# Half of one gate's products in bf16 parts, in four recurrent steps of eight

## The chip, the cores and the metric

One Trainium2 chip, one of its cores. The metric is the device time of one launch in microseconds; the kernel before was run three times and the median is taken. A profile is one more execution of the same program, recorded by the hardware.

## What is computed

The reference is a gated recurrent cell over 512 time steps, 8 sequences and 512 units, all in fp32, with the input added to the output at the end:

```
def step(h, x_t):
    fused = sigmoid(concat([x_t, h]) @ w_W + w_b)      # (8, 1024) @ (1024, 1024)
    hidden_state, output_state = split(fused, 2)        # r and z, 512 columns each
    memory_state = x_t @ wx_W + wx_b + hidden_state * (h @ wh_W + wh_b)
    h_new = output_state * h + (1.0 - output_state) * tanh(memory_state)
    return h_new, h_new
_, hs = scan(step, h0, swapaxes(x, 0, 1))
return x + swapaxes(hs, 0, 1)
```

Step i needs all 512 units of h from step i-1, so the steps cannot overlap as a whole. The products with x do not depend on h and can be made ahead.

## The kernel before

**Layout.** The 512 units stand as 4 blocks of 128 partitions. The stationary operand of every product with h is one block k of the state (32 columns: 4 steps of 8 sequences share a tile, and the current step fills 8 of the 32). The moving operand is a piece of the weights. The output goes to one quarter of 32 partitions of a PSUM bank: `tile_position` (0, 32j) with j = 0 to 3. So each product is four matmuls, one for each quarter j of the tensor array's columns, and the four quarters work side by side. A profile counts two records (two weight loads and two streams) for each fp32 matmul.

**Banks.** The 384 output columns of a step lie in three banks. A (192 columns) holds h, z and r for the first half of the units ("half A"); B (128 columns) holds r and h for half B; C (64 columns, in the tile `cs`) holds z for half B. On the tensor engine (PE) a step runs in this order, where the letter is the bank and the digit the block k of the state:

```
ORDER = "A0 B0 A1 A2 A3 B1 B2 B3 C0 C1 C2 C3"
```

After C3 come the products with x that belong to later steps (`x_step`, tiles `xp` and `eps`). They are spread over the steps by a table: in steps u = 0 to 3 of every eight, each quarter of the array takes 384 columns of them, in steps u = 4 to 7 it takes 288.

**The rest of a step.** The vector engine (DVE) transposes each piece out of PSUM (`tr`, `md1`, `tz`), the scalar engine (ACT) applies the sigmoids and tanh, and DVE scans compute the memory state (`m`) and the new state. The new state has four pieces, one for each block k: `update(0, 0)` and `update(0, 1)` write blocks 0 and 1 (tile hTA), `update(1, 0)` and `update(1, 1)` blocks 2 and 3 (tile hTB). A0 and B0 of the next step wait for block 0, A1 for block 1, A2 for block 2, A3 for block 3. GpSimd (POOL) adds x to the new state for the output (`ot`) and makes sums of x (`sx`).

**Seeding.** Before a group of four steps starts, its banks are filled with the x products and the bias: `spread` copies them with ACT, bank C by one copy of 64 columns in step u = 7 (for even groups) or u = 1 (for odd ones). All four steps of a group add their h products to the same region, each in rows of its own.

**Order.** The program is written in order by hand. `Flow` records the instructions, and its `plan` gives each one the semaphore waits that its reads, its writes and the PSUM banks require, within one engine too. The order on each engine is that of the code.

## Time and profile before

| | |
|---|---|
| median of 3 runs | 1654.62 us (1654.59 to 1654.87) |
| the profiled execution's own time | 1657.46 us, span 1655.7 us |
| busy in the span | PE 1645.6, PE weight loads 1500.2, DVE 1153.9, ACT 1193.8, POOL 301.9 us |
| PE matmul records | 54298, as many weight loads |
| granted PE clock | 0.999 |

Times in the rows are microseconds from the start of the span; the last number of a group's row is the mean of one instruction in ns. Matmul records overlap: a record's length includes the way through the array, so the distance from one start to the next tells how long the array was taken up. "PEld" is the weight load. A bracket at a row's end names what the engine waited for just before. Where two shapes of a step are compared, u is the step's place in its eight.

### The profile page before, as it was taken

The numbers are of one execution on the slowest core, as the hardware profiler recorded it, in microseconds if no ns is written. First come the engines' busy times: TensorE is split into PE (matmuls) and PEld (weight loads), VectorE is DVE, ScalarE is ACT, GpSimd is POOL, SyncE is SP. The second block draws the span as 40 slices with busy tenths as digits, with TensorE's granted clock in tenths as the row PEclk, the third lists the DMA queues.
The fourth block names the chain that finished last, engine by engine and source line by source line (L and its number), as shares of the span: only waits on it lengthen the run. The fifth ranks groups of instructions, "written<-read, shape, count | busy, mean of one in ns | idle before, by whom it ended". The sixth has DMA issues, their size and how long they took to land.

```text
span 1655.7 us, 125580 instructions
## 1 busy us (share of the span) xinstructions
PE 1645.6 (99%) x54298; PEld 1500.2 (91%) x54298; DVE 1153.9 (70%) x9194; ACT 1193.8 (72%) x5998; POOL 301.9 (18%) x1279
## 2 busy tenths in 40 slices
PE   9999999999999999999999999999999999999998
PEld 5999999999999999999999999999999999999987
DVE  6776676676766766767667767677676766766765
ACT  3777777777777777777777777777777777777775
POOL 1211111111111111111111111111111111111111
PEclk9999999999999999999999999999999999999999
DMA  4000000000000000000000000000000000000000
GB/s 182 11 18 14 15 15 16 16 14 15 16 15 15 14 16 16 14 14 15 16 15 14 14 17 14 15 14 17 14 14 15 17 14 14 15 17 10 10 10 10
DMA packets 37284, 31.14 MB, mean 19 GB/s; under 512 B 4084, under 2 KB 35060, under 8 KB 36600
## 3 DMA queue, kind: packets, MB, share of 16 engines
q1 hardware_dynamic: 36576, 22.89, 4.5%
q8 instruction: 424, 6.95, 1.7%
q14 instruction: 132, 1.08, 0.2%
q10 hardware_dynamic: 152, 0.22, 0.1%
HBM read 14.70 MB, written 8.39 MB: 14 GB/s over the span
## 4 chain that ended last, share of the span: by engine, by line
PE 99%; DVE 1%; issue 0%; ACT 0%; DVEq 0%; SPq 0%
PE A L227 40%; PE B L227 26%; PE xp L227 18%; PE cs L227 13%; PE eps L227 1%; DVE tr L227 0%; DVE m L227 0%; DVE tz L227 0%; DVE md1B L227 0%; DVE md1A L227 0%; DVE hTA L227 0%; DVE hTB L227 0%; ACT hTB L227 0%; DVE zeros L227 0%; DVE rows L227 0%
## 5 line engine op out<-in xcount | busy, mean ns | idle before, releaser
L227 PE MATMUL A<-wa,hTA 128*32 128x192 f32 x8192 | 559.5, 326 | 2.4 <-DVE hTA L227 2.2
L227 PE MATMUL B<-wb,hTA 128*32 128x128 f32 x8192 | 454.8, 273 | 0.0
L227 PE MATMUL A<-wa,hTB 128*32 128x192 f32 x8192 | 448.6, 326 | 0.0
L227 PEld LDWEIGHTS A<-wa,hTA 128*32 128x32 f32 x8192 | 292.5, 122 | 124.6 <-DVE hTA L227 101.7
L227 DVE STREAM_TRANSPOSE tr<-A 128x64 f32<-128x64 f32 x512 | 128.0, 250 | 367.6 <-PE A L227 367.6
L227 POOL TENSOR_TENSOR ot<-xin,hTB 128x16 f32<-128x16 f32 x495 | 123.8, 250 | 1290.4 <-DVE hTB L227 1290.4
L227 PEld LDWEIGHTS B<-wb,hTA 128*32 128x32 f32 x8192 | 352.6, 122 | 2.8 <-issue 0.3
L227 PE MATMUL B<-wb,hTB 128*32 128x128 f32 x8192 | 339.6, 273 | 0.0
L227 PEld LDWEIGHTS A<-wa,hTB 128*32 128x32 f32 x8192 | 330.4, 122 | 9.1 <-DVE hTB L227 0.2
L227 ACT ACTIVATE md0A<-tr 128x16 f32<-128x16 f32 x512 | 112.4, 219 | 238.5 <-DVE tr L227 238.4
L227 PE MATMUL xp<-tw,sx 128*32 128x384 f32 (+2 forms) x1464 | 269.7, 433 | 0.0
L227 PEld LDWEIGHTS B<-wb,hTB 128*32 128x32 f32 x8192 | 262.3, 122 | 0.2 <-issue 0.2
L227 PE MATMUL cs<-wb,hTB 128*32 128x64 f32 x8192 | 230.3, 219 | 0.4 <-issue 0.3
L227 PE MATMUL cs<-wb,hTA 128*32 128x64 f32 x8192 | 230.2, 219 | 0.0
L227 DVE TENSOR_TENSOR_SCAN hTB<-hd0B,hTB 128x24 f32<-128x24 f32 x1024 | 158.0, 196 | 99.8 <-ACT hTB L227 99.8
L227 PE MATMUL xp<-wx,xin 128*32 128x384 f32 (+4 forms) x1348 | 219.1, 413 | 0.0
L227 PEld LDWEIGHTS cs<-wb,hTA 128*32 128x32 f32 x8192 | 207.5, 122 | 0.0
L227 DVE TENSOR_TENSOR_SCAN hTA<-hd0A,hTA 128x24 f32<-128x24 f32 x1024 | 190.9, 186 | 0.0
L227 ACT ACTIVATE hd0B<-tz 128x16 f32<-128x16 f32 x512 | 115.6, 226 | 94.5 <-DVE tz L227 94.5
L227 PEld LDWEIGHTS cs<-wb,hTB 128*32 128x32 f32 x8192 | 180.2, 122 | 0.7 <-issue 0.7
L227 ACT ACTIVATE hTB<-hTB 128x16 f32<-128x16 f32 x512 | 120.3, 235 | 79.1 <-DVE hTB L227 72.8
L227 ACT ACTIVATE hTA<-m 128x8 f32<-128x8 f32 x1024 | 160.8, 206 | 0.6 <-DVE m L227 0.3
(101 smaller groups left out, 2680.6 us busy)
## 6 DMA issues: line engine op xcount, KB each, us to landing
out_dram<-ot SPq DMA_DIRECT2D x128, 64.0 KB, 1.6
xin<-in_x_dram SPq DMA_DIRECT2D x112, 64.0 KB, 2.4
wx<-in_wx_dram SPq DMA_DIRECT2D x4, 768.0 KB, 7.0
wa<-in_wa_dram SPq DMA_DIRECT2D x4, 384.0 KB, 9.8
wb<-in_wb_dram SPq DMA_DIRECT2D x1, 1152.0 KB, 13.7
xin<-in_x_dram SPq DMA_DIRECT2D x3, 256.0 KB, 3.7
wb<-in_wb_dram SPq DMA_DIRECT2D x1, 384.0 KB, 14.1
head<-in_xh_dram ACTq DMA_DIRECT2D x1, 208.0 KB, 4.7
```

What stands on the lines that cost most here:

```text
L227: inst = getattr(self, item.op, getattr(engine, item.op, None))(*item.args, **item.kw)
```

## The change

For half B of z the change takes the fp32 product apart into bf16 parts, in the steps u = 0 to 3 from step 8 on (252 of the 512 steps: the ones where `in_parts` holds). Three parts of the state (`split`: the high 16 bits of h, of what is left, and of what is left then; 8 columns each) stand side by side as one stationary operand of 24 columns. Three parts of the weights (`wb`, `w2`, `w3`, each read as the high 16 bits of every fp32 word, so with a step of two bf16 elements) stream past it. `kept` issues a matmul that loads no weights of its own but uses those that the matmul ahead of it has loaded. Each quarter and each block k has one loading matmul and two kept ones.

The nine products land in 24 rows and are summed afterwards: each such step has a PSUM region of its own (`cell`), DVE transposes it (`tzB`) and reduces over the four row groups (`tzs`). Since a sum over all rows must hold the x product once, `spread_c` seeds a cell through a mask that keeps the eight rows of the step: four ACT instructions of 64 columns for each even group, two in u = 6 and two in u = 7, in place of one copy. POOL makes the parts of the state by two subtractions for each half, before the output's additions; it makes `w2` and `w3` once, in steps 1 to 4. On DVE the first scan of `m` for half B now stands ahead of the z work, and `update(0, 1)` behind it. The state tiles of the two halves become one tile `hs` with 32 more rows of zeros.

```
-DVE_FILL = 23
+DVE_FILL = 14
...
+    hs = [const.tile([P, NQ, 64, 3], F32, name=f"hT{i}") for i in range(NH)]
+    split = [const.tile([P, NQ, 3, B], F32, name=f"split{i}") for i in range(2)]
+    w2 = const.tile([P, NQ, NQ, HU], F32, name="w2")
+    w3 = const.tile([P, NQ, NQ, HU], F32, name="w3")
+    mask = const.tile([P, GS, 32], F32, name="mask")
...
+    def parts(out_, i, k, j):
+        lhsT = high(split[i % 2])[:, k].rearrange("p u b -> p (u b)")[:, 1::2]
+        for n, t_ in enumerate((wb[:, k, j, :HU], w2[:, k, j], w3[:, k, j])):
+            (nc.tensor.kept if n else mm)(out_, lhsT, high(t_)[:, 1::2])
...
+    def cell(i):
+        return cs[:, HU * (i % GS) : HU * (i % GS) + HU] if i // GS % 2 == 0 else banks[1]["C"]
+    def in_parts(i):
+        return NH <= i < T and i // GS % 2 == 0
+    def spread_c(g, steps_):
+        for s in steps_:
+            nc.scalar.activation(
+                cell(GS * g + s), source(g)[:, XP["C"]], AF.Copy, scale=mask[:, s, :1]
+            )
...
             for j in range(NQ):
-                mm(ps[bank][32 * j : 32 * j + 32, :], hs, wh(bank, k, j))
+                if bank == "C" and in_parts(i):
+                    parts(cell(i)[32 * j : 32 * j + 24], i, k, j)
+                else:
+                    to = cell(i) if bank == "C" else ps[bank]
+                    mm(to[32 * j : 32 * j + 32, :], lhsT, wh(bank, k, j))
...
+            if hf and in_parts(i):
+                tz = work.tile([P, 2, B], F32, tag="tzs", name=f"tzs_{i}")
+                nc.vector.tensor_reduce(
+                    tz, tzb[0].rearrange("p c (u b) -> p c b u", u=4), mybir.AxisListType.X, ALU.add
+                )
...
+        if in_parts(i):
+            tzb = [work.tile([P, 2, 32], F32, tag="tzB", name=f"tzB_{i}")]
+            nc.vector.transpose(tzb[0].rearrange("p c n -> p (c n)"), raw["z"][1])
+            memory(1, 0)
+            turn_z(1)
+            update(0, 1)
+            memory(1, 1)
...
+        if nxt and u in (6, 7):
+            spread_c(2 * o + 2, (2 * u - 12, 2 * u - 11))
         for hf in range(2):
             act(state(hf, i + 1, 0), state(hf, i + 1), AF.Copy)
+            if in_parts(i + 1):
+                ks, s1 = slice(2 * hf, 2 * hf + 2), B * ((i + 1) % GS)
+                t_, new = split[(i + 1) % 2][:, ks], hs[(i + 1) % NH][:, ks]
+                nc.gpsimd.tensor_tensor(
+                    t_[:, :, :2].rearrange("p k u b -> p k b u"),
+                    new[:, :, s1 : s1 + B, 2].unsqueeze(3).broadcast_to([P, 2, B, 2]),
+                    high(new).rearrange("p k (u n) s -> p k n u s", u=2)[:, :, s1 : s1 + B, :, 5],
+                    ALU.subtract,
+                )
+                nc.gpsimd.tensor_tensor(t_[:, :, 2], t_[:, :, 0], high(t_)[:, :, 0, 1::2], ALU.subtract)
...
-            spread(2 * o + 2, "C")
```

Three places show how the order moves. The first is PE in a step u = 1 in mid-program, from the C products over the x products (`xp`) to the next step's A products. Before:

```order
L227 MATMUL cs<-wb,hTA_68 32x64 x8
L227 MATMUL cs<-wb,hTB_76 32x64 x8
L227 MATMUL xp_122<-wx,xin_140 32x384 x2
L227 MATMUL xp_122<-tw_101,sx_107 32x384 x2
L227 MATMUL A_118<-wa,hTA_69 32x192 x4
```

After, with the first of sixteen groups of three (`w_77` and `w_78` are `w2` and `w3`):

```order
L245 MATMUL B_117<-wb,hT_68 32x128 x12
L245 MATMUL cs<-wb,split_76 24x64
L219 MATMUL cs<-w_77,split_76 24x64
L219 MATMUL cs<-w_78,split_76 24x64
...
L245 MATMUL xp_120<-wx,xin_131 32x384 x2
L245 MATMUL xp_120<-tw_99,sx_105 32x384 x2
L245 MATMUL A_116<-wa,hT_69 32x192 x4
```

Sixteen fp32 matmuls of 64 columns became sixteen groups of one loading and two kept matmuls; the x products behind them are as many as before.

The second is DVE in a step u = 2, from the transposes of bank B to the new state. Before:

```order
L227 STREAM_TRANSPOSE tr_2_145<-B_119 128x64
L227 STREAM_TRANSPOSE md1B_89<-B_119 128x64
L227 SCALAR_TENSOR_TENSOR hTA_70<-hd0A_91,hTA_69 128x24
L227 STREAM_TRANSPOSE tz_2_146<-cs 128x64
L227 SCALAR_TENSOR_TENSOR hTA_70<-hd0A_91,hTA_69 128x24
L227 SCALAR_TENSOR_TENSOR m_2_142<-md0B_85,md1B_89 128x16 x2
L227 SCALAR_TENSOR_TENSOR hTB_78<-hd0B_93,hTB_77 128x24 x2
```

After (the four pieces of the state are all in `hT`; `hd0A` and `hd0B` tell the half):

```order
L245 STREAM_TRANSPOSE tr_2_143<-B_117 128x64
L245 STREAM_TRANSPOSE md1B_86<-B_117 128x64
L245 SCALAR_TENSOR_TENSOR hT_70<-hd0A_88,hT_69 128x24
L245 STREAM_TRANSPOSE tzB_156<-cs 128x64
L245 SCALAR_TENSOR_TENSOR m_2_140<-md0B_82,md1B_86 128x16
L245 TENSOR_REDUCE tzs_157<-tzB_156 128x16
L245 SCALAR_TENSOR_TENSOR hT_70<-hd0A_88,hT_69 128x24
L245 SCALAR_TENSOR_TENSOR m_2_140<-md0B_82,md1B_86 128x16
L245 SCALAR_TENSOR_TENSOR hT_70<-hd0B_90,hT_69 128x24 x2
```

The second piece of half A's state stands two instructions later, behind one scan of `m` and the added reduce.

The third is POOL at the end of the steps u = 0 and u = 1, after (`hT_69` is the state that step u = 1 makes). Before, the two additions `ot` stood there alone:

```order
L245 TENSOR_TENSOR sx_108<-xin_145,sx_104 128x64
L245 TENSOR_TENSOR ot_124<-xin_138,hT_68 128x8x2 x2
L245 TENSOR_TENSOR split_75<-hT_69 128x2x8x2
L245 TENSOR_TENSOR split_75<-split_75 128x2x8
...
L245 TENSOR_TENSOR ot_124<-xin_138,hT_69 128x8x2 x2
```

Two pairs of subtractions (the second pair reads as the first) were put ahead of the additions; the first pair waits for half A's state, the second for half B's.

## The prediction

> **What bounds the kernel now.** I read the page's first part and its chain of waits, then the stretch of the steady steps:

> ```profile
> PE 1645.6 (99%) x54298; PEld 1500.2 (91%) x54298; DVE 1153.9 (70%) x9194; ACT 1193.8 (72%) x5998; POOL 301.9 (18%) x1279
> PE 99%; DVE 1%; issue 0%; ACT 0%; DVEq 0%; SPq 0%
> 98.00:1600.00 1502.00, 1501.92 (x49891) 1380.11 (x49887) 1050.81 (x8414) 1104.75 (x5529) 275.70 (x1174) 1.00 0.05 15
> ```

> PE is never idle there (1501.92 of 1502 us), at the full clock (1.00). A busy PE is not yet a PE at its peak, so I look at the length of a step, by the first DVE transpose of two steps u = 1, 2 and two steps u = 5, 6:

> ```profile
> 789.13 0.25 DVE L227 STREAM_TRANSPOSE tr<-A 128x64 f32<-128x64 f32 x1 [0.86 <-PE A L227]
> 792.39 0.25 DVE L227 STREAM_TRANSPOSE tr<-A 128x64 f32<-128x64 f32 x1 [1.13 <-PE A L227]
> ...
> 802.03 0.25 DVE L227 STREAM_TRANSPOSE tr<-A 128x64 f32<-128x64 f32 x1 [0.97 <-PE A L227]
> 805.14 0.25 DVE L227 STREAM_TRANSPOSE tr<-A 128x64 f32<-128x64 f32 x1 [0.28 <-PE A L227]
> ```

> A step takes 3.26 us with the longer x products and 3.11 with the shorter. What the streams alone need follows from how a record's length grows with its columns:

> ```profile
> L227 PE MATMUL A<-wa,hTA 128*32 128x192 f32 x8192 | 559.5, 326 | 2.4 <-DVE hTA L227 2.2
> ...
> L227 PE MATMUL cs<-wb,hTA 128*32 128x64 f32 x8192 | 230.2, 219 | 0.0
> L227 PE MATMUL xp<-tw,sx 128*32 128x384 f32 x976 | 205.7, 486 | 0.0
> ```

> (486 - 219) / 320 = 0.834 ns a column. A quarter of the array streams in one step 8 records for each bank (384 columns together) and two of 384 columns: (8 x 384 + 2 x 384) x 0.834 = 3.20 us, in 26 records. 3.26 leaves 2.3 ns a record. So the streams fill the step, and time taken from them is time gained, as long as the new state is not late. This is one step u = 1 on PE:

> ```profile
> 789.52 0.40 PE L227 MATMUL cs<-wb,hTA 128*32 128x64 f32 x15
> ...
> 789.97 0.49 PE L227 MATMUL xp<-wx,xin 128*32 128x384 f32 x1
> ...
> 790.61 0.55 PE L227 MATMUL A<-wa,hTA 128*32 128x192 f32 x8
> 790.94 0.44 PE L227 MATMUL B<-wb,hTA 128*32 128x128 f32 x8
> 791.16 0.55 PE L227 MATMUL A<-wa,hTA 128*32 128x192 f32 x8
> 791.48 0.88 PE L227 MATMUL A<-wa,hTB 128*32 128x192 f32 x16
> ```

> C takes 0.45 us (789.52 to 789.97), the x products 0.64; A0 starts at 790.61, A1 at 791.16, A2 at 791.48.

> **Term 1: the C products.** Out go 8 fp32 records of 64 columns in each quarter, 0.45 / 8 = 56 ns each: 53.4 of stream (64 x 0.834) and 2.6 besides. In come 12 bf16 records of 64 columns. [...]

> ```profile
> 2.68 0.37 PE L227 MATMUL A<-none 128*128 128x192 bf16 x1
> 2.84 0.31 PE L227 MATMUL B<-none 128*128 128x128 bf16 x1
> 2.95 0.37 PE L227 MATMUL A<-none 128*128 128x192 bf16 x1
> 3.11 3.67 PE L227 MATMUL xp<-zeros 128*128 128x512 f32 x4
> ...
> L227 PE MATMUL xp<-zeros 128*128 128x512 f32 x4 | 3.7, 1074 | 0.0
> ```

> From 2.68 to 2.95, 320 bf16 columns pass: 0.84 ns each. The fp32 records of 512 columns follow each other in some (3.67 - 1.07) / 3 = 0.87 us: 1.69 ns a column. A bf16 record costs half an fp32 one, so at full clock 0.417 ns a column and 26.7 + 2.6 = 29.3 ns. 12 x 29.3 = 0.351 us against 0.448: **97 ns saved in each of 252 steps, 24.4 us**. Bounds: with no cost besides the stream 12 x 26.7 = 0.320, 128 ns, 32 us; the dear end is in the rivals. I take 29.3, since the 2.6 stands in every row that I can check.

> Do the four quarters still work side by side, when three matmuls in a row go to one quarter? An fp32 matmul already gives its quarter two records, and at the turn from block 1 to block 2 a step u = 2 shows:

> ```profile
> 793.01 0.22 PE L227 MATMUL cs<-wb,hTB 128*32 128x64 f32 x1
> 793.02 0.22 PE L227 MATMUL cs<-wb,hTA 128*32 128x64 f32 x1
> ```

> A product of the later block (hTB) starts in one quarter before the last of the earlier block (hTA) starts in another. The quarters do not wait for each other's order. [...]

> **Term 2: is the new state in time?** DVE and ACT in the same step (first DVE from bank B's transpose, then ACT):

> ```profile
> 789.86 0.23 DVE L227 STREAM_TRANSPOSE tr<-B 128x64 f32<-128x64 f32 x1
> ...
> 790.14 0.20 DVE L227 TENSOR_TENSOR_SCAN hTA<-hd0A,hTA 128x24 f32<-128x24 f32 x1
> 790.26 0.23 DVE L227 STREAM_TRANSPOSE tz<-cs 128x64 f32<-128x64 f32 x1
> 790.41 0.17 DVE L227 TENSOR_TENSOR_SCAN hTA<-hd0A,hTA 128x24 f32<-128x24 f32 x1
> 790.50 0.25 DVE L227 TENSOR_TENSOR_SCAN m<-md0B,md1B 128x16 f32<-128x16 f32 x2
> 790.94 0.31 DVE L227 TENSOR_TENSOR_SCAN hTB<-hd0B,hTB 128x24 f32<-128x24 f32 x2 [0.20 <-ACT hTB L227]
> ...
> 790.52 0.22 ACT L227 ACTIVATE hd0B<-tz 128x16 f32<-128x16 f32 x1 [0.18 <-DVE tz L227]
> 790.70 0.31 ACT L227 ACTIVATE hTB<-m 128x8 f32<-128x8 f32 x2
> ```

> and the hand-over from a scan to PE where PE did wait, in step 1:

> ```profile
> 24.84 0.20 DVE L227 TENSOR_TENSOR_SCAN hTA<-hd0A,hTA 128x24 f32<-128x24 f32 x1
> ...
> 25.10 0.55 PE L227 MATMUL A<-wa,hTA 128*32 128x192 f32 x8 [0.24 <-DVE hTA L227]
> ```

> The scan ends at 25.04 and PE starts at 25.10: 0.06. After the change, in this step's times: A0 is due at 790.51 (0.10 earlier), A1 at 791.06, A2 at 791.38, A3 at 791.70.
> - Block 0 is as before: 790.34 + 0.06 = 790.40, 0.11 ahead.
> - `tzB` at 790.26; the scan of `m` at 790.41; the reduce needs `tzB` (790.49), starts at about 790.53 and takes some 0.20. That is an estimate: a 128x16 scan takes 0.17 to 0.20, a 64-element transpose 0.23; 0.15 to 0.30 as bounds. It ends at 790.73.
> - Block 1's scan follows it on DVE at 790.67, ends at 790.84: A1 from 790.90, 0.16 ahead.
> - The sigmoid of z from 790.77 to 790.99 (the ACT row starts 0.03 after its transpose ends). Block 2's scan, until now held by tanh until 790.94, starts at 791.03 and ends at 791.22: A2 from 791.28, 0.10 ahead. With a reduce of 0.30 it would just meet it.
> - The second tanh follows the sigmoid, to about 791.15; block 3's scan to 791.38: A3 from 791.44, 0.26 ahead.

> All are covered. DVE has nothing else to do until A's transpose: the row at 792.39 waited 1.13 us, and of that 0.12 goes to the later scans and 0.10 to the shorter step.

> **Term 3: POOL.** Two pairs of subtractions a step, of 32 and 16 elements, against these rows:

> ```profile
> 791.33 0.25 POOL L227 TENSOR_TENSOR ot<-xin,hTB 128x16 f32<-128x16 f32 x1 [2.75 <-DVE hTB L227]
> ...
> 795.01 0.32 POOL L227 TENSOR_TENSOR sx<-xin 128x64 f32<-128x64 f32 x1
> ```

> 16 elements 0.25, 64 elements 0.32, so 32 about 0.27, and 1.1 us a step into 2.75 of idle time. The parts of block 3 are ready about 0.7 us after its scan, 792.1; C2 of the next step comes at 793.0. That cover is large. The danger is elsewhere: the first subtraction starts about 0.08 after block 1's scan (as `ot` does: 791.25 to 791.33), at 790.92, so it is at work when block 2's scan wants to start (791.03). Where a POOL and a DVE operation with two SBUF inputs met, in the first steps:

> ```profile
> 35.83 0.25 POOL L227 TENSOR_TENSOR ot<-head,hTA 128x16 f32<-128x16 f32 x1
> 38.71 0.47 POOL L227 TENSOR_TENSOR ot<-head,hTB 128x16 f32<-128x16 f32 x1 [2.63 <-DVE hTB L227]
> ...
> 35.91 0.57 DVE L227 TENSOR_TENSOR tw<-wx,tw 128x384 f32<-128x384 f32 x1
> 38.55 0.53 DVE L227 TENSOR_TENSOR tw<-wx,tw 128x384 f32<-128x384 f32 x1
> ```

> With DVE first (38.55), POOL's 0.25 became 0.47. With POOL first (35.83), DVE's 0.53 became 0.57: DVE lost 0.04, not the 0.17 that POOL still had to run. So block 2's scan loses some 0.04 of its 0.10. [...]

> I allow 1 us for steps where the margins are thinner than here.

> **Edits costed at little.** `spread_c` gives ACT two instructions of 64 columns in u = 6 and in u = 7, three more than before in eight steps; ACT is busy 72% and would be late only for the next step's first sigmoid. The longer fills at the start lie under the first weights' transfers. `w2` and `w3`, sixteen POOL operations in steps 1 to 4, meet the `tw` rows of DVE there: 0.5 us in all, as an allowance. PE's added waits on POOL stand before C0 and C2 with the cover named.

> **Sum.** -24.4 + 1 + 0.5 = -22.9. The profiled execution took 1657.46, 2.84 above the median, so it would become 1634.6; from the median 1654.62 I get **1632**.

> **Rivals.**
> [...]
> - *No change:* each group's fresh weights are not hidden behind three short streams, and the first record of each block keeps the 56 ns of today. Then 4 x (56 + 58.6) = 0.458 against 0.448: +2.6 us, **1657**. For it: every load in the trace has a 56 ns stream or longer to hide behind. Against it: half as many loads, and of 24 columns, not 32.
> - *Slower, by the stride:* the weights are read at every second bf16 element; every moving operand of the trace is contiguous or a repeated element, so no row has the price. If it halves the rate, a record costs 53.4 + 2.6 = 56 ns, C takes 12 x 56 = 0.67, +0.224 us a step: +56 us, **1711**. It decides from 37 ns a record on (0.448 / 12). [...]
> - *Slower, by the order:* each group of three holds up the next quarter: 16 x 2 x 29.3 = 0.94 us and more for C, +0.5 a step, **near 1780**. The 793.01 rows speak against it.

> That the change does not do what it says would be that the kept matmuls load weights all the same: it costs as "no change" does.

> **How the numbers follow.** Forecast 0.60, half gain 0.12, no change 0.08, stride 0.10, order 0.06, and 0.04 for other losses on the new path through POOL and the reduce. Faster by over 0.2% (3.3 us, about what a measurement here can tell from nothing): 0.60 + 0.12 = 0.72; the same: 0.08; slower: 0.20. The likeliest case alone spans 1622 (no cost besides the stream) to 1640; with half gain and no change the range is 1622 to 1658, which leaves the 0.20 of the slower cases out.

> **What would show it.** Steps u = 0 to 3 of 3.16 us and u = 4 to 7 still of 3.11; the first record of C to the first x product 0.35 us apart; three records for each load in C; no waits of A1 or A2 for DVE beyond a few hundredths; hTB scans no longer than 0.20. The prediction is wrong if C still takes 0.45 or more, or if A2 waits for a scan that a subtraction delayed.

## The result, and the profile after

| | before, us | after, us | ratio (95% interval) |
|---|---|---|---|
| first measurement, 12 runs each | 1654.70 | 1650.63 (1649.37 to 1653.5) | 0.9976 (0.9967 to 0.9985) |
| profiled execution, span | 1655.7 | 1649.9 | |
| once more, on a second chip | 1657.77 | 1659.74 (1654.83 to 1663.07) | 1.0010 (1.0001 to 1.0019) |

The change is worth 4.1 us of the 22.6 forecast on the first chip, and nothing on the second, where it is 2.0 us slower. Three lines of the page of the changed kernel: busy times, shares of the chain that ended last, and PE's instruction queue (packets, MB, share of 16 engines).

```profile
PE 1637.8 (99%) x58330; PEld 1394.7 (85%) x50266; DVE 1241.6 (75%) x9443; ACT 1256.4 (76%) x6190; POOL 542.0 (33%) x2304
...
PE 98%; DVE 1%; ACT 0%; issue 0%; DVEq 0%; SPq 0%
...
q8 instruction: 425, 6.96, 1.7%
```

PE is still the chain. Against the kernel before there are 4032 matmuls more and 4032 loads fewer, so in C three records now share a load; the sum, 108,596 records, is that of before. DVE has 88 us more, ACT 63 and POOL 240. The same window as before (busy us of PE, PEld, DVE, ACT, POOL):

```profile
98.00:1600.00 1502.00, 1500.97 (x53864) 1286.52 (x46308) 1135.06 (x8687) 1166.59 (x5730) 495.91 (x2127) 1.00 0.06 15
```

The granted clock is still 1.00. Now the lengths of steps, by the first DVE transpose of steps u = 1, 2, 3, 4 and then 5, 6:

```profile
786.84 0.25 DVE L245 STREAM_TRANSPOSE tr<-A 128x64 f32<-128x64 f32 x1 [0.55 <-PE A L245]
790.02 0.25 DVE L245 STREAM_TRANSPOSE tr<-A 128x64 f32<-128x64 f32 x1 [0.80 <-PE A L245]
793.36 0.25 DVE L245 STREAM_TRANSPOSE tr<-A 128x64 f32<-128x64 f32 x1 [0.17 <-PE A L245]
796.55 0.25 DVE L245 STREAM_TRANSPOSE tr<-A 128x64 f32<-128x64 f32 x1
...
799.66 0.25 DVE L245 STREAM_TRANSPOSE tr<-A 128x64 f32<-128x64 f32 x1 [0.97 <-PE A L245]
802.77 0.25 DVE L245 STREAM_TRANSPOSE tr<-A 128x64 f32<-128x64 f32 x1 [0.28 <-PE A L245]
```

The differences are 3.18, **3.34**, 3.19 and 3.11 us, and 3.11 for u = 5. Steps with parts are shorter than the 3.265 of before, except u = 2, which is longer. That is so in 61 of the 63 groups of eight. Medians over the run for u = 0, 1, 2, 3: 3.183, 3.184, 3.332, 3.181; for u = 4 to 7 3.105 to 3.110, as before.

The products themselves, as groups of the changed kernel (out<-in, shape, count | busy us, mean ns | idle us before):

```profile
L245 PE MATMUL cs<-wb,hT 128*32 128x64 f32 x8320 | 169.3, 219 | 0.0
L219 PE MATMUL cs<-w,split 128*24 128x64 bf16 x8064 | 135.2, 192 | 0.6 <-issue 0.6
L245 PE MATMUL cs<-wb,split 128*24 128x64 bf16 x4032 | 127.2, 193 | 0.3 <-issue 0.2
```

A bf16 record is 219 - 192 = 27 ns shorter than an fp32 one of the same 64 columns. C, from its first record to the first x product, takes 0.447 us before and 0.36 after (medians), so 0.087 less; the medians of the steps u = 0, 1 and 3 are 0.081 to 0.084 lower.

**Where the step u = 2 loses it.** PE's loads, its first matmuls of C, and then ACT, at the turn from u = 1 to u = 2:

```profile
789.61 0.77 PEld L245 LDWEIGHTS B<-wb,hT 128*32 128x32 f32 x24
790.55 0.39 PEld L245 LDWEIGHTS cs<-wb,split 128*24 128x24 bf16 x16 [0.17 <-issue]
```

```profile
790.58 0.22 PE L245 MATMUL cs<-wb,split 128*24 128x64 bf16 x4
```

```profile
789.24 0.23 ACT L245 ACTIVATE hT<-hT 128x16 f32<-128x16 f32 x1 [0.15 <-DVE hT L245]
789.48 0.47 ACT L245 COPY more<-eps 64x384 f32<-64x384 f32 x1
789.97 0.33 ACT L245 COPY A<-odd 128x192 f32<-128x192 f32 x1
790.23 0.21 ACT L245 COPY cs<-odd 128x64 f32<-128x64 f32 x1
790.46 0.22 ACT L245 ACTIVATE md0A<-tr 128x16 f32<-128x16 f32 x1
```

The profile names no releaser for the 0.17 us ("issue"), but C0 of this step waits, in the program, for ACT's last access to the bank `cs`. That access is the copy that seeds the *odd* group's C cell, which lies in the same bank as the cells of the even group. It ends at 790.44; C0's loads start at 790.55 and its first matmul at 790.58, so the hand-over from the copy to the matmul takes 0.14. The same place in the kernel before, ACT and then PE:

```profile
791.53 0.47 ACT L227 COPY more<-eps 64x384 f32<-64x384 f32 x1
792.02 0.32 ACT L227 COPY A<-odd 128x192 f32<-128x192 f32 x1
792.28 0.21 ACT L227 COPY cs<-odd 128x64 f32<-128x64 f32 x1
```

```profile
792.79 0.40 PE L227 MATMUL cs<-wb,hTA 128*32 128x64 f32 x15
```

There the copy ended at 792.49, 0.30 ahead of C's first matmul; with a hand-over of 0.14, some 0.16 was free. From the first transpose of the step on, the copies began at 2.40 (791.53 - 789.13) and now begin at 2.64 (789.48 - 786.84), and C is due 0.09 earlier. That makes 0.24 + 0.09 - 0.16 = 0.17 too late. The waits of PE's loads, before and after (us, times, longest):

```profile
PEld cs L227 <- issue: 0.7, 2, 0.5
```

```profile
PEld cs L245 <- issue: 13.0, 65, 0.6
```

Of the 65, 58 are in steps u = 2.

**And a second loss, scattered.** A step u = 3 at 589.8 us, PE:

```profile
589.99 0.22 PE L219 MATMUL cs<-w,split 128*24 128x64 bf16 x2
590.63 0.19 PE L219 MATMUL cs<-w,split 128*24 128x64 bf16 x1 [0.42 <-issue]
```

In the middle of C nothing starts for 0.6 us, and no engine is waited for. I count such stalls by what a step has over the median of its u, in steps 9 to 499: 2.0 us in all before (7 steps over 0.06 us), **7.3 us after (29 steps)**.

The balance for the span: 252 x -0.083 = -20.9; u = 2 is 0.149 above the other steps with parts, x 63 = +9.4; scattered stalls +5.3; start and end +0.3 (the first eight steps 0.8 longer, the way to them and the end 0.5 shorter). Sum -5.9, against -5.8 measured.

### The profile page after: what moved, and what is told of

Same layout as the page of the kernel before. It is cut to its first block, busy times and chain, and to the rows that moved or that the text cites. A ratio compares the mean times of both kernels' runs of the same rounds, so it can differ in the third digit from the quotient of the medians.

```text
span 1649.9 us, 127364 instructions
## 1 busy us (share of the span) xinstructions
PE 1637.8 (99%) x58330; PEld 1394.7 (85%) x50266; DVE 1241.6 (75%) x9443; ACT 1256.4 (76%) x6190; POOL 542.0 (33%) x2304
## 3 DMA queue, kind: packets, MB, share of 16 engines
q8 instruction: 425, 6.96, 1.7%
## 4 chain that ended last, share of the span: by engine, by line
PE 98%; DVE 1%; ACT 0%; issue 0%; DVEq 0%; SPq 0%
PE A L245 41%; PE B L245 27%; PE xp L245 17%; PE cs L245 9%; PE cs L219 4%; PE eps L245 1%; DVE m L245 0%; DVE tr L245 0%; DVE tw L245 0%; DVE hT L245 0%; DVE md1A L245 0%; DVE tz L245 0%; DVE md1B L245 0%; DVE even L245 0%; ACT cs L245 0%
## 5 line engine op out<-in xcount | busy, mean ns | idle before, releaser
L245 PE MATMUL A<-wa,hT 128*32 128x192 f32 x16384 | 872.5, 327 | 3.7 <-DVE hT L245 3.7
L245 PEld LDWEIGHTS A<-wa,hT 128*32 128x32 f32 x16384 | 547.9, 122 | 192.8 <-DVE hT L245 134.0
L245 PE MATMUL B<-wb,hT 128*32 128x128 f32 x16384 | 653.1, 273 | 0.0
L245 PEld LDWEIGHTS B<-wb,hT 128*32 128x32 f32 x16384 | 542.8, 122 | 21.2 <-DMA wb<-in_wb_dram 0.9
L245 POOL TENSOR_TENSOR ot<-xin,hT 128x16 f32<-128x16 f32 x991 | 225.4, 252 | 594.4 <-DVE hT L245 592.5
L245 ACT ACTIVATE hT<-m 128x8 f32<-128x8 f32 x2048 | 350.5, 208 | 77.9 <-DVE m L245 68.1
L245 ACT ACTIVATE hT<-hT 128x16 f32<-128x16 f32 x1024 | 217.0, 225 | 60.3 <-DVE hT L245 57.7
L245 DVE TENSOR_TENSOR_SCAN hT<-hd0B,hT 128x24 f32<-128x24 f32 x1024 | 180.9, 205 | 74.7 <-ACT hT L245 50.7
L245 DVE TENSOR_TENSOR_SCAN hT<-hd0A,hT 128x24 f32<-128x24 f32 x1024 | 199.0, 194 | 0.0
L245 PE MATMUL cs<-wb,hT 128*32 128x64 f32 x8320 | 169.3, 219 | 0.0
```

What stands on the lines that cost most here:

```text
L245: inst = getattr(self, item.op, getattr(engine, item.op, None))(*item.args, **item.kw)
```

## Experiments

Each was compared with the kernel before on the same chip; the chips differ by up to 3 us for that kernel. "Over the medians" is the count of stalls as above.

| run | us | before there | ratio (95%) | over the medians, us (steps) |
|---|---|---|---|---|
| C copy first | 1653.67 | 1657.54 | 0.9981 (0.9972 to 0.9990) | 10.0 (37) |
| fp32 products | 1659.83 | 1657.54 | 1.0010 (1.0001 to 1.0019) | 3.7 (14) |
| round robin | 1660.55 | 1657.54 | 1.0018 (1.0010 to 1.0027) | 13.3 (54) |
| balanced | 1713.59 | 1657.54 | 1.0337 (1.0323 to 1.0352) | 8.9 (33) |
| after, again | 1659.74 | 1657.77 | 1.0010 (1.0001 to 1.0019) | 13.8 (60) |
| C between the copies | 1646.89 | 1657.77 | **0.9934 (0.9922 to 0.9947)** | 8.3 (36) |
| 64 more at the start | 1657.99 | 1657.77 | 0.9999 (0.9990 to 1.0007) | 12.5 (51) |
| two parts | 1650.36 | 1657.77 | 0.9948 (0.9935 to 0.9961) | 7.2 (33) |
| before, again | 1656.81 | 1656.97 | 0.9998 (0.9989 to 1.0007) | 4.1 (13) |
| C between, again | 1647.41 | 1656.97 | **0.9935 (0.9921 to 0.9948)** | 9.4 (34) |
| 16 more a step | 1679.76 | 1656.97 | 1.0130 (1.0117 to 1.0144) | 19.1 (67) |
| C between, round robin | 1646.79 | 1656.97 | 0.9935 (0.9923 to 0.9947) | 8.6 (41) |

### Which copy is late: the C copy first

```diff
 elif u == 1:
+    spread(2 * o + 1, "C")
     if sums:
         nc.scalar.copy(more[HI], eps)
-    spread(2 * o + 1, "BC" if o == 0 else "AC")
+    spread(2 * o + 1, "B" if o == 0 else "A")
```

> Only the order of ScalarE's copies in steps u = 1 changes: the seed of the odd group's C cell goes first, then the copy to more, then the seed of A. Theory (the late copy into the bank that holds the C cells is what C0 of u = 2 waits for): the wait of 0.16 us before C0 in every step u = 2 is gone, its period falls from 3.33 to 3.18 (up to 3.22 if md0A, still late by 0.2 us, now shows), 63 x 0.15 = 9.5 us less than the changed kernel: 1641 us, 1639 to 1644. Rival (C0 waits for something else, the parts of block 0 from POOL or its own instructions): u = 2 stays at 3.33 and the time at 1650.6.

The wait before C0 of u = 2 is gone (waits for "issue" at `cs`: 1.4 us in 6 places). So the late copy was its cause. But A to C of u = 3 now takes 2.286 us and not 2.173, so of 9.4 us only about 3 are won by the medians, and the stalls take as much away (10.0 us over the medians, 7.3 in the first profile of the changed kernel). ACT, DVE and PE's loads of that step:

```profile
789.35 0.32 ACT L245 COPY A<-odd 128x192 f32<-128x192 f32 x1
789.67 0.22 ACT L245 ACTIVATE md0A<-tr 128x16 f32<-128x16 f32 x1
```

```profile
789.29 0.25 DVE L245 STREAM_TRANSPOSE tr<-A 128x64 f32<-128x64 f32 x1 [0.82 <-PE A L245]
...
789.93 0.28 DVE L245 TENSOR_TENSOR_SCAN m<-md0A,md1A 128x16 f32<-128x16 f32 x2
...
790.78 0.27 DVE L245 TENSOR_REDUCE tzs<-tzB 128x16 f32<-128x64 f32 x1
...
791.34 0.40 DVE L245 TENSOR_TENSOR_SCAN hT<-hd0B,hT 128x24 f32<-128x24 f32 x2
...
792.55 0.25 DVE L245 STREAM_TRANSPOSE tr<-A 128x64 f32<-128x64 f32 x1 [0.16 <-PE A L245]
...
793.10 0.28 DVE L245 TENSOR_TENSOR_SCAN m<-md0A,md1A 128x16 f32<-128x16 f32 x2
```

```profile
791.61 0.51 PEld L245 LDWEIGHTS A<-wa,hT 128*32 128x32 f32 x16 [0.17 <-DVE hT L245]
```

ACT still has the same three copies, so `md0A` is late by 0.09 us (the scan of `m` starts 0.64 after the transpose, in the next step 0.55), everything behind it shifts, and A2 waits for block 2's scan. I had put the price of this at up to 0.04; it is 0.11, since A2 has no margin (below).

### The other half alone: fp32 products

All of the seeding, splits and weight parts stay; C, DVE's order and the sigmoid of z are as before.

```diff
-                if bank == "C" and in_parts(i):
+                if False:
...
-            if hf and in_parts(i):
+            if False:
...
-        if in_parts(i):
+        if False:
             tzb = ...
```

> The seeding of four cells, the splits on POOL and the parts of the weights stay as in the changed kernel; the products of C, the order on DVE and the sigmoid of z are those of the kernel before. Theory: C takes 0.447 us in all steps, the copy ends before C0 of u = 2, no wait there; steps u = 0 to 3 of 3.265, the start 0.8 us longer: 1655.5 us (1654.5 to 1656.5), and the scattered stalls of PE are as rare as before (about 8 steps, 2 us). Rival (what the new path costs lies in the splits on POOL and the copies on ScalarE, not in the products): u = 2 still waits or the stalls are as many as in the changed kernel (27 steps, 6 us): 1660 to 1665.

C is 0.447 in every step, u = 0 to 3 are 3.265 with no wait in u = 2, and the stalls are few. So the copies and POOL's work do not lose the time of u = 2 by themselves; the shorter C and the later state uncover it. It lies 2.3 us above the kernel before (0.2 to 3.1 by the interval), somewhat more than the 0.8 expected. Its scans of `hT` (hd0B) take 201 ns on average with POOL's subtractions beside them, 196 in the kernel before and 205 in the changed kernel. The kernel before, this one, and the changed kernel with its reduce and its first subtraction:

```profile
L227 DVE TENSOR_TENSOR_SCAN hTB<-hd0B,hTB 128x24 f32<-128x24 f32 x1024 | 158.0, 196 | 99.8 <-ACT hTB L227 99.8
```

```profile
L245 DVE TENSOR_TENSOR_SCAN hT<-hd0B,hT 128x24 f32<-128x24 f32 x1024 | 163.0, 201 | 100.0 <-ACT hT L245 100.0
```

```profile
L245 DVE TENSOR_TENSOR_SCAN hT<-hd0B,hT 128x24 f32<-128x24 f32 x1024 | 180.9, 205 | 74.7 <-ACT hT L245 50.7
...
L245 DVE TENSOR_REDUCE tzs<-tzB 128x16 f32<-128x64 f32 x252 | 68.3, 271 | 0.1
```

```profile
L245 POOL TENSOR_TENSOR split<-hT 128x32 f32<-128x32 f32 x504 | 131.3, 261 | 432.1 <-DVE m L245 420.3
```

### Spreading the copies: a miss, then a version that holds

```diff
 elif u == 1:
+    spread(2 * o + 1, "C")
     if sums:
         nc.scalar.copy(more[HI], eps)
-    spread(2 * o + 1, "BC" if o == 0 else "AC")
+    if o == 0:
+        spread(1, "B")
 elif u == 2:
...
     if o:
-        spread(2 * o + 1, "B")
+        spread(2 * o + 1, "A")
 elif u == 3:
+    if o:
+        spread(2 * o + 1, "B")
```

> ScalarE's copies of the odd group spread out: u = 1 has the seed of C and the copy to more, u = 2 the seed of A, u = 3 the seed of B. Theory: the wait of C0 in u = 2 is gone as in e1 (9.5 us), and md0A of the next step is on time too, which is worth 0 to 0.04 us in 63 steps: 1639 to 1641 us, 0 to 2.5 us below e1. Rival (md0A of u = 2 is covered, or the copies only move the lateness to u = 3 and 4): as e1, or 2 to 5 us above it.

u = 2 and u = 3 are 3.182 and 3.181: with ACT unloaded both waits are gone. But the step after them costs 1.15 us more:

```profile
PEld B L245 <- ACT B L245: 79.0, 62, 1.4
```

B0 is the second block of u = 4 in the order, and its seed was now copied at the end of u = 3. I had looked at ACT's load and not at which product needs the seed first.

The copy of C moved alone, between the two copies of the new state:

```diff
 elif u == 1:
...
-    spread(2 * o + 1, "BC" if o == 0 else "AC")
+    spread(2 * o + 1, "BC" if o == 0 else "A")
 for hf in range(2):
     act(state(hf, i + 1, 0), state(hf, i + 1), AF.Copy)
+    if hf == 0 and u == 2 and 0 < o < LAST:
+        spread(2 * o + 1, "C")
```

> ScalarE's copy that seeds the odd group's C cell moves from the end of u = 1 to u = 2, between the two copies of the new state; u = 1 keeps the copies to more and A. Theory (ScalarE has room for 0.75 us of copies after a step with parts and had 0.98 in u = 1; that made C0 of u = 2 late, and, with the copy first, md0A and through it A2 of u = 3): both waits go, u = 2 and u = 3 fall to 3.18, the medians of the eight steps sum to 25.16 and not 25.31: 9 to 10 us below after_again, less what the stalls differ by (up to 3 us). Rival (the wait moves once more, to C0 of u = 3 or to the next step's first sigmoid): 3 us below, as with the copy first.

```profile
787.68 0.22 ACT L245 ACTIVATE hT<-hT 128x16 f32<-128x16 f32 x1
787.79 0.21 ACT L245 COPY cs<-odd 128x64 f32<-128x64 f32 x1
788.05 0.23 ACT L245 ACTIVATE hT<-hT 128x16 f32<-128x16 f32 x1
788.29 0.47 ACT L245 COPY even<-xp 64x384 f32<-64x384 f32 x1
788.67 0.26 ACT L245 COPY B<-odd 128x128 f32<-128x128 f32 x1
789.13 0.22 ACT L245 ACTIVATE md0A<-tr 128x16 f32<-128x16 f32 x1 [0.20 <-DVE tr L245]
```

The copy stands where ACT was waiting for DVE, ACT is idle again before `md0A`, and C0 of u = 3 loads at 789.13 without a wait. All four steps are 3.18 to 3.19 (medians 3.180, 3.186, 3.181, 3.182). Against the changed kernel on the same chip it takes 12.9 us less; the profiled spans differ by 14.7, 9.6 by the medians and 5.5 by fewer stalls. This version beats both kernels. Once more, on another chip, where it gave the same ratio to the kernel before:

> The kernel with the copy between the two copies of the new state, once more, as the measure for the next two. All theories: medians of the steps u = 0 to 3 of 3.18, and 0.5% to 0.8% below the kernel before on the same chip; 6 to 10 us over the medians.

The medians came out at 3.179 to 3.185.

### How much the state had left: two parts

```diff
-for n, t_ in enumerate((wb[:, k, j, :HU], w2[:, k, j], w3[:, k, j])):
+for n, t_ in enumerate((wb[:, k, j, :HU], w2[:, k, j])):
```

> Two of the weights' three parts instead of three (the last part's products are left out): 8 bf16 records in each quarter for C. Theory (30 ns a record, and behind it a state that is just in time): C to the first x product falls from 0.36 to 0.24 in u = 0 to 3, but A0 and A2 then wait for the state: the period falls by 0.03 to 0.09, not by 0.12, 8 to 20 us below after_again. Rival 1 (C is limited by the loading of weights, not by the records): C stays near 0.33, up to 8 us less. Rival 2 (the state has room): the whole 0.12, 29 us less.

This kernel leaves out the products with the third part of the weights. C is 0.24: four records in each quarter are 0.12 us, 30 ns each. But u = 0 and 1 take 3.165 and 3.195, against 3.185 and 3.186 with three parts: of the 8.1 us between the profiled spans the medians of the eight steps give 1.5 in all, and 6.6 are fewer stalls (7.2 us over the medians against 13.8). The loads of A, u = 3:

```profile
790.63 0.19 PEld L245 LDWEIGHTS A<-wa,hT 128*32 128x32 f32 x8 [0.49 <-DVE hT L245]
791.19 0.19 PEld L245 LDWEIGHTS A<-wa,hT 128*32 128x32 f32 x8
791.59 0.51 PEld L245 LDWEIGHTS A<-wa,hT 128*32 128x32 f32 x16 [0.21 <-DVE hT L245]
```

A2 waits for the state, as in the first experiment. At C = 0.36 the state is just in time; a C shorter than that gains almost nothing.

### The order of a block's twelve matmuls

```diff
-for j in range(NQ):           # three in a row to quarter j
-    parts(cell(i)[32 * j : 32 * j + 24], i, k, j)
+for n in range(3):            # part n to all four quarters
+    for j in range(NQ):
+        parts(cell(i)[32 * j : 32 * j + 24], i, k, j, n)
```

> In C the twelve matmuls of a block go round the four quarters (four that load weights, then four and four that keep them) and not three in a row to one quarter. Theory (the quarters work side by side in either order; the 0.36 us are 12 records of 30 ns): C to the first x product stays at 0.36 and the time at 1650.6 (1649 to 1652). Rival 1 (three in a row hold up the next quarter by a little): C falls to 0.33 or less, 252 x 0.03 = 7 us less, 1643. Rival 2 (the kept ones have to find their weights again): C rises towards 0.45, 1660 to 1672.

C stays at 0.36. The time came out 6.9 us above the kernel with the C copy first on the same chip; 2.7 of that are the two kernels' different copies (by the medians), 3.3 stalls. That left the order's part open, so it was tried again on the better version:

> As e5_again, with the twelve matmuls of a block of C going round the four quarters. Theory (the order is free; the 7 us that the first round-robin kernel lay above the one with the copy first were the other kernel's order of copies and the chance of the stalls): within 3 us of e5_again, C at 0.36. Rival (the order makes pieces of instructions run out more often): 4 to 8 us above e5_again, with half as much time again over the medians.

0.6 us below, C 0.36, as many stalls. In this kernel the order is free.

### The scattered stalls

The trace counts PE's records in order, and each packet of PE's instruction queue is 16 KB: 6.96 MB for 108,596 records are 64 bytes a record, 256 records a packet. I call the 256 records of a packet a piece, and the place in a stalled step where the next record starts late the jump. Of the 29 stalled steps after, 16, with 4.4 of 6.4 us, have their jump at the 187th to 194th record, counted in 256s from the start of the trace, so I take the pieces to change there. At 590.63 above, the packet came from 588.20 to 589.07; it started 1.9 us after PE had entered the piece before, where the usual is 0.7.

```diff
 warm()
+for n in range(32):
+    mm(xps[1][:, :1], none, none[:, :1])
```

> The changed kernel once more, beside the next three on the same chip. All theories: 3 to 5 us below the kernel before; medians of the steps as in its first profile (u = 0, 1, 3 3.18, u = 2 3.33). Theory on the scattered stalls (PE's instructions come in pieces of 256 and a piece comes late): they stand again at the 193rd instruction of a piece, most of them in C or the x products, 4 to 10 us in all, though not in the same steps. Rival (they belong to the work or to transfers of x and of the output): the same steps stall, at any place in a piece.

> 32 matmuls of one column (64 instructions of PE) more at the start, while PE waits for the first data; all else as in the changed kernel. Theory (pieces of 256 instructions, fetched late): the stalls stand at the same place in a piece, the 193rd, which is another place of the program; medians of the steps unchanged; the time within 3 us of after_again, up or down. Rival (the stalls belong to the work): they keep their steps, and their place in a piece moves by 64.

In the changed kernel, again, 33 of 60 stalled steps (8.8 of 13.0 us) jump at the same records of a piece; with 64 records more at the start 33 of 51 (9.2 of 11.5 us), still there, so at other places of the program; one step alone has such a jump in both runs. So these stalls belong to the ends of pieces and not to the work.

Not all stalls are of this kind. Steps 41, 136, 163, 258 and 448 stall in all three of these profiles (the changed kernel twice, and with 64 records more), for about 1 us together, and with the 64 records their place in a piece moves along (110 to 174 for step 136). There DVE idles 0.15 to 0.22 us before a scan of `m` for half B or before the reduce, and A1 waits for the state behind it. Step 258, DVE and then PE's loads:

```profile
842.34 0.19 DVE L245 TENSOR_TENSOR_SCAN m<-md0B,md1B 128x16 f32<-128x16 f32 x1 [0.19 <-issue]
```

```profile
842.85 0.19 PEld L245 LDWEIGHTS A<-wa,hT 128*32 128x32 f32 x8 [0.18 <-DVE hT L245]
```

In all five it is the same place in DVE's own records counted in 256s (63, from 0, in the first profile of the changed kernel), so the end of a piece of DVE may be the cause; no run moved it. The other 22 of the 60 stalled steps, with some 3 us, no run explains.

Over all these runs PE hardly ever enters a piece earlier than 2.2 us after its packet starts. The forecast of 3 to 5 us below the kernel before failed here: this chip gave 13.8 us over the medians, and that ate the gain (the kernel before was not profiled on it).

```diff
         (nc.tensor.kept if n else mm)(out_, lhsT, high(t_)[:, 1::2])
+    nc.tensor.kept(out_[:, :1], lhsT, none[:, :1])
```

> The kernel before once more, with a profile on this chip. Theory (the stalls at the ends of PE's pieces come with the shorter C, and more of them on some chips): few stalls, 5 to 12 steps and 2 to 4 us over the medians of their u, beside 7 us or more of the kernels with parts on the same chip. Rival (a slower chip stalls either kernel alike): 25 or more steps and 6 us or more.

> As e5_again, and after the three matmuls of each quarter one more of a single column of zeros, which keeps the weights: 16 instructions more of PE in each step with parts (228 for 212), nearly no work. Theory (a piece of 256 instructions has to last until the next has come): the medians of u = 0 to 3 grow by 0.02 to 0.07 (5 to 18 us in all), and besides these the stalls at the ends of pieces grow, by half or more: from 6 to 10 us over the medians to 10 to 20. Rival (the number of instructions has nothing to do with the stalls): the medians grow alike and the time over the medians stays at 6 to 10 us.

On one chip: 4.1 us (13 steps) for fp32 products, 9.4 (34) with parts, 19.1 (67) with 16 records more a step, 46 of the 67 at ends of pieces. The waits of PE's loads in the two kernels with parts, without and with the 16:

```profile
PEld cs L245 <- issue: 1.8, 5, 0.5
```

```profile
PEld cs L245 <- issue: 8.4, 24, 0.8
```

So in this pair more records make more stalls. That fewer records make fewer is not shown: two parts had 7.2 us, but C between the copies, with all the records, had 8.3 on the same chip. Nor can the number alone be it, since the kernel before and the changed kernel have the same 108,596 records; in the changed kernel those of C follow each other faster. What else is not settled: a piece lasts 3.7 to 3.9 us in the median in all these kernels, but the packet starts later after the piece before was entered: 0.53 to 0.61 us (median) in the kernels with fp32 products, 0.68 to 0.80 in those with parts. Why the start moves, no run shows. The medians of the 16-more kernel also grew by 0.10 a step, 25 us, where 0.02 to 0.07 was expected: a matmul of one column costs about as much as one of 64 (below).

## Why the prediction was right or wrong, point by point

- **The bound** was right: PE is the chain in both, at a granted clock of 1.00.
- **Term 1** was sized a little high, and its reason is open. 97 ns were forecast; C shrank by 87 and the steps by 83, so 20.9 us came where 24.4 were forecast. A record takes 30 ns (0.36 / 12), not 29.3. But the term had 26.7 of these as the stream of 64 columns, and a kept record of a single column costs 25 ns too (16 more a step). So what sets the 30 ns is not shown, and that the sum came so close may be luck. Stride 2 does not halve the rate (that would be 56 ns a record), and three records share a load, so the rivals "no change" and "slower, by the stride" are out. That a bf16 column takes half of an fp32 one was read from the first 7 us, 0.84 for 1.69 ns. The 1.69 is twice the 0.834 of the steady steps, though the granted clock was 1.00 there too (kernel before, 2.6 to 7.0 us); why, no run shows. So 0.417 ns in the steady steps was an estimate of the author's.
- **Side by side** was right: in bursts or round the quarters, C is 0.36. Bursts that hold up the next quarter would have given 0.94 or more, by the prediction's reckoning.
- **Term 2** held in its outcome, not in its margins. In the steps that follow a step on time, A1 and A2 cost next to nothing: the medians of u = 0, 1 and 3 are within 6 ns of the 3.178 that the shorter C alone would give. But the reduce takes 0.27 us (of 0.15 to 0.30 allowed, 0.20 taken), which ate 0.07 of A2's 0.10, and what was left is about 0.02 or less: after the steps with parts the loads of A2 start 0.05 after block 2's scan ends (median; 0.17 before), which is the hand-over itself. So a `md0A` 0.09 late (C copy first) or a C 0.12 shorter (two parts) turned into waits at A2 almost in full.
- **Term 3** was right in its outcome. The means of the rows, 205 for 196 ns, mix several cases. Of the scans of block 2 in the steps 16 to 499 of the changed kernel, 183 start while a subtraction is at work that has about 0.16 us still to run; they take 216 ns and the others 208. So 8 ns are lost and not the 40 allowed. The half gain (1643 us, chance 0.12) has block 2's scan wait until the subtraction ends; no run shows such a wait, only the 8 ns.
- **The step that failed is "edits costed at little".** It said that ACT "would be late only for the next step's first sigmoid", and looked at u = 6 and 7, where copies were added. It missed that in u = 1 the copy of the odd C cell, unchanged in the text, lies in the bank which C0 of the next step needs; that the reduce and the later scans push ACT's copies back; and that C comes 0.09 earlier. The copy ended 0.30 us ahead of C before (792.49, 792.79), some 0.16 of it free after the hand-over, and the rows stood in the trace. Worth 9.4 us: moving that one copy gave 9.6 us in the medians. "Who waits for that" was asked for the instructions added, not for those moved.
- **The second miss is a term that was not in the sum:** the scattered stalls, most of them at the ends of PE's instruction pieces. Before, it was 2.0 us in 7 steps, which the view of waits shows only as part of its "issue" rows, and I read past those. They cost 5.3 us more on the first chip, and with 13.8 us on the second they take all that was left of the gain.
- **The start:** the first eight steps lost 0.8, where 0.5 was allowed. That the way to them and the end came out 0.5 shorter is no effect that a run shows; the first transpose of `tr` stands anywhere from 17.8 to 19.8 us in the profiles.
- **The sum:** -22.9 was forecast for -5.9 in the balance. Of these 17.0 us, 9.4 are the wait at C0, 5.3 the stalls and 3.5 the size of term 1; the allowances of 1.5 took 0.3. The time on the first chip lies within 1622 to 1658, but by none of the cases that the range was made of: that is luck.
- **What would show it:** steps of 3.18 for 3.16, 0.36 for 0.35, u = 4 to 7 at 3.11, three records a load; the scans of `hT` (hd0B) 0.205 on average for "no longer than 0.20". The list of what would make it wrong named C at 0.45 or A2 behind a subtraction. Neither happened; a wait at C0 was not on it.

## What to carry to other kernels

When a product gets shorter, everything that was just in time for its start gets late: list, for each wait of that first instruction, when its releaser ends in the trace, bank neighbours included, and move each by what the change adds before it. Shortening one product pays only down to where the next wait ends, which one run with the product cut further shows at once (here 1.5 us of 30). And where a kernel is a stream of records of a few tens of ns, count PE's records as a cost of their own (here 25 ns for one of a single column).
